# Splitting the second product of the first two down-projection units, and the last product of all by columns

## The chip, the cores and the metric

The kernel runs on one core of a Trainium2 chip. The time is device time in microseconds (us) of one execution, from three runs: median 447.69 us, 447.19 to 448.56. All matrix products are in float32.

## The reference, cut to what matters

```python
xn = layernorm(x)                       # x: (2, 1024, 512) float32
s  = s4_convolution(xn)                 # a causal convolution along the 512 features
h1 = xn @ w1.T + 2 * (xn @ A1.T) @ B1.T # 512 -> 1376, with a rank-16 addition
h3 = xn @ w3.T + 2 * (xn @ A3.T) @ B3.T
g  = silu(h1) * h3
d  = g @ w2.T + 2 * (g @ A2.T) @ B2.T   # 1376 -> 512, the down projection
out = x + s * silu(d)
```

The layer norm has no weights. The filter of the convolution is itself computed from small inputs (`Lambda`, `p`, `q`, `Vc`, `Ct`, `B`, step), a long chain of small operations.

## The kernel before, in words

The rank-16 additions are merged into the weights, so that each projection is one matrix product. Each product is done by Strassen-Winograd: a 2 by 2 block product in seven block products instead of eight, with sums of blocks made on VectorE (DVE) or GpSimd (POOL) beforehand and partial results added afterwards. The first projection (lines up to L1237) does this twice over and writes `g` to DRAM in chunks of 128 hidden rows (`store_g`, L802).

The change is in the second part, the down projection. The tokens are cut into pairs of 128 (token tiles), eight `unit`s in all (L1293). The hidden dimension has eleven chunks: ten in five pairs, and a short last one of 96 rows, `gl`. A unit makes two output tiles `o0` and `o1` of 128 tokens by 512 columns, each in two halves of 256 columns (`lo`, `hi`), from seven products. In the order of the code, by their Winograd names:

- P1 = `a11`·`b11`, into the PSUM bank `xb`, copied by ScalarE (ACT) to `z1` (L1312)
- P2 = `a12`·`b21` plus `gl`·`wl0`, into `wb`; DVE adds `z1` and gets `o0[:, lo]` (L1326)
- P6 = `s2`·`t2`, accumulated into `xb`, copied to `z2`
- P7 = `s3`·`t3` plus a product with `gl`, into `yb`
- P5 = `s1`·`t1`, accumulated into `xb`, copied to `z4`; DVE adds `yb` and gets `o1[:, hi]` (L1340)
- P3 = `s4_`·`b22` plus a product with `gl`, accumulated into `xb`, which ScalarE takes through silu into `o0[:, hi]`
- P4 = `a22`·`t4` plus a product with `gl`, accumulated into `yb`; DVE adds `z2` and gets `o1[:, lo]` (L1369)

P4 writes the bank `yb` that the addition of L1340 reads. A product of five pairs of chunks is ten matmul records of 256 columns in the profile (a float32 product has two); with `gl` it is twelve.

The engines' queues are in order, and the order is the one in which the code issues. `run` (L1386) takes the units in turn: each round advances one unit to its next `yield`, then issues one item of a list of block sums (`parts`), then, from round `s4_from` on, `s4_steps` steps of the filter's computation (`s4_work`). So a sum or a filter step that DVE gets in one round stands ahead of everything that a later round gives it. The first two units run together, with sixteen parts: the sums `t1` (two pieces), `s1` (two), `s4_` (two), `t4` (two), then eight sums for the next group of tokens, group 1, made from a load `g<-g_dram` (L1147; the tile is `g2`). The filter's steps begin with round 5, four in a round. Units 2 and 3 follow in the same way with eight steps a round; from unit 4 on the convolution (L922) is done beside the projection.

With `wait=True` (the first two units alone) P1 is issued in two parts: the first four chunks of both units, and then the fifth, because chunks 8 and 9 of `g` come from DRAM last (`room<-g_dram`). So in the kernel before, the rounds are: P1's four chunks (units 0, 1), P1's fifth chunk, P2, P6, P7, P5, P3, P4.

The last unit ends with P3 alone: after the product ScalarE takes `silu`, DVE multiplies with the convolution (L1289), adds `x` (L1290), and the half tile is stored by a DMA on SP's queue (L1291). The convolution's bank needs a late addition of `m` (L1288) before its upper half is used; `result` does it when the columns asked for end at 512.

Of the kernel before, what the change touches and what calls it, by code (L numbers as in the profile page):

```python
# [17 lines left out]
P = 128  # L18
DIM = 512
# [12 lines left out]
HALF = DIM // 2  # L32
# [75 lines left out]
def s4_gated_ffn(  # L108
# [59 lines left out]
    def bank(tag, borrow=False):  # L168

        i = turn[tag]  # L170
        if not borrow:
            turn[tag] = 1 - i
        return psum.tile([P, 512], F32, tag=f"{tag}{i}", name=tag, bufs=1)
# [571 lines left out]
    def product(ps, pairs, first, parts=1):  # L745
        n = ps.shape[1] // parts
        for part in range(parts):
            cols = slice(part * n, (part + 1) * n)
            for i, (lhsT, rhs) in enumerate(pairs):
                nc.tensor.matmul(  # L750
                    ps[:, cols],
                    lhsT=lhsT,
                    rhs=rhs if parts == 1 else rhs[:, cols],
                    start=first and i == 0 and part == 0,
                    stop=i == len(pairs) - 1,
                    skip_group_check=True,
                )
# [51 lines left out]
    class Gate:  # L809
# [12 lines left out]
        def silu(self, o, c, src):  # L822
            nc.scalar.activation(c, c if src is None else src, AF.Silu)  # L823
            self.c[o] = c
            self.pair_up()
# [89 lines left out]
    def conv_product(lhs, x01, sb, tok, tag):  # L915

        y, m_ps = bank(tag), bank("w")[:, :P]
        x0, x1, x2, x3 = (lhs[i][:, sb, k, tok] for i in range(2) for k in range(2))
        k = [conv[:, n * P : (n + 1) * P] for n in range(5)]

        def mul(to, x_, by, start=False):
            nc.tensor.matmul(  # L922
                to, lhsT=x_, rhs=by, start=start, stop=True, skip_group_check=True
            )

        mul(m_ps, x01[:, sb, tok], k[2], True)
        m = work.tile([P, P], F32, tag="m", name="m", bufs=3)
        nc.scalar.copy(m, m_ps)
        mul(y[:, : 2 * P], x0, conv[:, : 2 * P], True)
        mul(y[:, 2 * P :], x2, conv[:, : 2 * P])  # L930
        mul(y[:, 3 * P :], x0, k[3])
        mul(y[:, P : 2 * P], x1, k[0])
        mul(y[:, 2 * P : 3 * P], x1, k[4])
        mul(y[:, 3 * P :], x3, k[0])
        return y, m


    def add_chain(n, ch, places=PLACES):
# [124 lines left out]
    for n, place in enumerate((12.1, 12.8, 13.7, 14.4)):  # L1063
        b, i = divmod(n, 2)
# [84 lines left out]
    def group_piece(grp, i, sums):  # L1149


        p, n = g_in[grp][i], (3, 2)[i]
        a11, a12, a21, a22 = (
            p[:, k : k + 2 * n - 1 : 2, m] for m in range(2) for k in range(2)
        )
        s2, s3, s4_ = (sums[:, j] for j in range(3))
        parts = [
            lambda t=t, op=op: nc.vector.tensor_tensor(*t, op)
            for t, op in (
                ((s3, a11, a21), sub),  # L1160
                ((s2, a22, s3), sub),
                ((a21, a21, a22), add),
                ((s4_, a12, s2), sub),
            )
        ]
        return (a11, a12, a22, a21, s2, s3, s4_), parts

    def operands(grp, pieces):

        return [*zip(*pieces), g_in[grp][1][:LASTR, LAST - 6]]  # L1170
# [71 lines left out]
    b11, b21, _, b22 = room["b"]  # L1242
# [8 lines left out]
    class Place:  # L1251
# [30 lines left out]
                nc.sync.dma_start(out=self.o[h], in_=o_dram[self.u, h])  # L1282

        def result(self, h, y, cols=slice(0, DIM), last=False):
            o, (y, m) = self.o[h][:, cols], y
            if cols.stop == DIM:
                late = y[:, HALF:].rearrange("p (n t) -> p n t", n=2)
                nc.vector.tensor_tensor(late, late, m.unsqueeze(1).broadcast_to([P, 2, P]), add)  # L1288
            nc.vector.tensor_tensor(o, o, y[:, cols], mult)  # L1289
            (nc.vector if last else nc.gpsimd).tensor_tensor(o, o, self.xin[h][:, cols], add)  # L1290
            nc.sync.dma_start(out=out[self.rows[h], cols], in_=o)  # L1291

    def unit(u, read, held=None, wait=False):  # L1293


        a11, a12, a22, s1, s2, s3, s4_, gl = read
        pl = Place(u)
        cut, last = pl.cut, u == UNITS - 1
        xb, wb, yb = (bank(tag)[:, :HALF] for tag in ("x", "w", "y"))
        pl.gates()  # L1300
        o0, o1 = pl.o
        if u >= HOLD:
            pl.load_in()
        lo, hi = slice(0, HALF), slice(HALF, DIM)

        def mul(ps, a, b, start=False, more=()):
            chunks = [t[:, c, cut] for t in a for c in range(t.shape[1])]
            product(ps, list(zip(chunks, b)) + list(more), start)

        def snapshot(name):  # L1310
            t = work.tile([P, HALF], F32, tag=name, name=name, bufs=2)
            nc.scalar.copy(t, xb)  # L1312
            return t

        if wait:
            pairs = [t[:, c, cut] for t in a11 for c in range(t.shape[1])]
            pairs = list(zip(pairs, b11))
            product(xb, pairs[:-1], True)
            yield
            product(xb, pairs[-1:], False)  # L1320
        else:
            mul(xb, a11, b11, True)
        z1 = snapshot("z1")
        yield
        mul(wb, a12, b21, True, [(gl[:, 0, cut], wl0)])
        nc.vector.tensor_tensor(o0[:, lo], z1, wb, add)  # L1326
        if held:
            held.result(0, held.conv(0, "aux"))
        yield
        mul(xb, s2, tw[1])  # L1330
        z2 = snapshot("z2")
        silu(o0[:, lo], o0[:, lo])
        if held:
            held.result(1, held.conv(1, "aux"))
        yield
        mul(yb, s3, tw[2], True, [(gl[:, 1, cut], wl1)])
        yield
        mul(xb, s1, tw[0])
        z4 = snapshot("z4")
        nc.vector.tensor_tensor(o1[:, hi], z4, yb, add)  # L1340
        p3 = xb, s4_, b22, False, [(gl[:, 0, cut], wl1)]
        p4 = yb, a22, tw[3], False, [(gl[:, 1, cut], wld)]
        if last:
            silu(o1[:, hi], o1[:, hi])
            y = [pl.conv(0, "aux"), pl.conv(1, "aux")]
            pl.result(1, y[1], hi)
            pl.result(0, y[0], lo)
            yield
            mul(*p4)
            nc.vector.tensor_tensor(o1[:, lo], z2, yb, add)  # L1350
            silu(o1[:, lo], o1[:, lo])
            yield
            mul(*p3)
            pl.result(1, y[1], lo)
            silu(o0[:, hi], xb)
            pl.result(0, y[0], hi, True)
            return
        y0 = pl.conv(0, "aux") if u >= HOLD else None
        yield
        mul(*p3)  # L1360
        silu(o0[:, hi], xb)
        if u >= HOLD:
            y1 = pl.conv(1, "aux")
            pl.result(0, y0)
        else:
            pl.set_aside(0)
        yield
        mul(*p4)
        nc.vector.tensor_tensor(o1[:, lo], z2, yb, add)  # L1369
        silu(o1, o1)  # L1370
        if u >= HOLD:
            pl.result(1, y1)
        else:
            pl.set_aside(1)

    def sums_room():
        return work.tile([P, 3, NPAIR, JW], F32, tag="s2", name="s2", bufs=2)

    def following(grp):
        sums = sums_room()  # L1380
        two = [
            group_piece(grp, i, sums[:, :, c]) for i, c in enumerate((slice(3), slice(3, NPAIR)))
        ]
        return operands(grp, [t[0] for t in two]), two[0][1] + two[1][1]

    def run(units, parts=(), s4_steps=0, s4_from=0):  # L1386

        units, parts = deque(units), deque(parts)
        for n in itertools.count():
            while units and next(units[0], units) is units:  # L1390
                units.popleft()
            if not units:
                break
            units.rotate(-1)
            if parts:
                parts.popleft()()
            for _ in range(s4_steps if n >= s4_from else 0):
                next(s4_work, None)
        for part in parts:
            part()  # L1400
# [3 lines left out]
    two = [group_piece(0, 0, room_), group_piece(0, 1, sums_room()[:, :, 3:])]  # L1404
    read = operands(0, [t[0] for t in two])
# [3 lines left out]
    s4_loads()  # L1409
    load_g(1, range(0, NHC, 2))  # L1410
    after_, more = following(1)
    run([unit(u, read, wait=True) for u in range(2)], [*t[:2], *s1, *s4_, *t[2:], *more], 4, 5)

    second_tokens()
    lhs = [[xr[:, 0], xr[:, 1]], [room["b12"], xr[:, 2]]]
# [13 lines left out]
    read = after_  # L1429
    load_g(2, range(0, NHC, 2))  # L1430
    after_, more = following(2)
# [9 lines left out]
    for u in range(HOLD, UNITS):  # L1441
# [5 lines left out]
        if j == 0:  # L1447
            read = after_
            if ahead:
                load_g(grp + 1, range(0, NHC, 2))  # L1450
        more = ()
        if ahead and j == 1:
            after_, more = following(grp + 1)
# [77 lines left out]
```

## Time and profile before

| what | us |
|---|---|
| median of three runs | 447.69 |
| the profiled execution, its own time | 447.56 |
| its span, first to last instruction | 445.8 |
| PE (TensorE) busy in the span | 438.9 |
| DVE busy | 292.0 |
| ACT busy | 137.4 |
| POOL busy | 202.2 |

The profile is of one execution. A row of a timeline has the start and length in us, the engine, the line of the code, the operation, the tile written and the tiles read, their shape, and in brackets how long the engine stood idle before it and what ended that. PE is a matmul, PEld a weight load, which overlaps it. Rows of one kind that follow each other are merged (x4). A matmul's end is modelled and reaches into the next one's, so a rate is read from starts. The two units' first matmuls of the down projection start at 269.85 us of the span, P4 of unit 0 at 300.04, and the last product at 438.99.

### The profile page before, as it was taken

Reading aid. Unit: us, or ns where it says so; the run is one execution under the profiler, and the core shown is the slowest. Engines: PE = TensorE matmul, PEld = TensorE weight load, DVE = VectorE, ACT = ScalarE, POOL = GpSimd, SP = SyncE. Lnnn points to the kernel's source line nnn. Section 1 sums busy time; section 2 is a strip of 40 time slices with the busy share of each in tenths; the row PEclk is TensorE's granted clock in tenths of the full one; section 3 lists DMA queues with packets and bytes.
Section 4 is the critical chain, followed back from the end, with each engine's and each line's share of the span. In section 5 each row is a group of like instructions: output and inputs, shape, how many; then the busy total and the mean of one; then the engine's idle time right before and its main releaser. Section 6 shows DMA issues by size and latency. Waiting matters only on the chain.

```text
span 445.8 us, 5022 instructions
## 1 busy us (share of the span) xinstructions
PE 438.9 (98%) x1678; PEld 272.2 (61%) x1678; DVE 292.0 (66%) x496; ACT 137.4 (31%) x279; POOL 202.2 (45%) x156
## 2 busy tenths in 40 slices
PE   8999999999999999999999999999999999999996
PEld 8635334344444444444443446888898999989995
DVE  5898999946874687368836887979892214541222
ACT  2776342453245334433443242111102101011110
POOL 1315169895679548944894379200000213221221
PEclk9999999999999999999999999999999999999999
DMA  8911304025002400340054536486803742323211
GB/s 263 361 53 46 118 0 147 24 73 165 25 24 97 140 24 24 112 145 24 24 184 147 165 126 199 143 308 205 330 1 114 282 136 76 120 96 94 94 49 47
DMA packets 35257, 53.52 MB, mean 120 GB/s; under 512 B 4640, under 2 KB 21344, under 8 KB 35104
## 3 DMA queue, kind: packets, MB, share of 16 engines
q1 hardware_dynamic: 35104, 53.07, 36.2%
q8 instruction: 13, 0.21, 0.2%
q10 hardware_dynamic: 128, 0.14, 0.1%
q14 instruction: 12, 0.10, 0.1%
HBM read 33.80 MB, written 19.40 MB: 119 GB/s over the span
## 4 chain that ended last, share of the span: by engine, by line
PE 93%; DMA 2%; DVE 1%; issue 1%; POOL 1%; ACT 0%; POOLq 0%; DVEq 0%; SPq 0%
PE x L750 44%; PE y L750 23%; PE w L750 12%; PE aux L922 6%; PE w L975 2%; DMA room<-g_dram 1%; PE aux L303 1%; PE aux L381 1%; PE y L381 1%; PE w L922 1%; PE y L527 1%; PE aux L709 1%; DMA g_dram<-s 0%; POOL s L831 0%; DVE t_in L1200 0%
## 5 line engine op out<-in xcount | busy, mean ns | idle before, releaser
L1290 POOL TENSOR_TENSOR o<-o,xin 128x512 f32<-128x512 f32 (+1 forms) x17 | 22.5, 1324 | 136.9 <-DVE o L1289 136.9
L831 POOL TENSOR_TENSOR s<-c,s 128x512 f32<-128x512 f32 (+1 forms) x44 | 63.6, 1451 | 16.6 <-ACT c L823 11.5
L770 ACT COPY s<-x 128x512 f32<-128x512 f32 (+1 forms) x54 | 31.6, 586 | 87.8 <-PE x L750 86.5
L750 PE MATMUL x<-t_in,s 128*128 128x512 f32 (+1 forms) x148 | 55.2, 500 | 0.0
L774 DVE TENSOR_TENSOR s<-s,y 128x512 f32<-128x512 f32 (+1 forms) x54 | 36.1, 680 | 17.1 <-PE y L750 10.9
L864 POOL TENSOR_TENSOR s<-ua_three,s 128x512 f32<-128x512 f32 x20 | 32.4, 1619 | 26.9 <-DVE s L774 26.9
L750 PEld LDWEIGHTS x<-t_in,s 128*128 128x128 f32 x148 | 26.8, 190 | 22.8 <-issue 12.5
L864 POOL TENSOR_TENSOR ua_three<-ua_three,s 128x512 f32<-128x512 f32 x20 | 33.0, 1650 | 13.6 <-DVE s L774 13.6
L750 PE MATMUL y<-t_in,s 128*128 128x256 f32 (+1 forms) x108 | 35.9, 459 | 0.0
L1312 ACT COPY z<-x 128x256 f32<-128x256 f32 x24 | 8.8, 372 | 79.9 <-PE x L750 79.9
L864 POOL TENSOR_TENSOR s<-u_three,s 128x512 f32<-128x512 f32 x20 | 28.5, 1425 | 1.8 <-ACT c L823 1.0
L823 ACT ACTIVATE c<-c 128x512 f32<-128x512 f32 x40 | 25.2, 632 | 8.8 <-DVE c L864 8.8
L750 PEld LDWEIGHTS y<-t_in,s 128*128 128x128 f32 x108 | 20.1, 190 | 11.5 <-issue 8.8
L788 ACT COPY w<-x 128x512 f32<-128x512 f32 (+1 forms) x37 | 21.1, 570 | 12.2 <-PE x L750 12.1
L922 PE MATMUL aux<-conv,xr 128*128 128x128 f32 (+1 forms) x128 | 23.2, 314 | 0.0
L1288 DVE TENSOR_TENSOR aux<-aux,m 128x256 f32<-128x256 f32 x16 | 6.9, 431 | 23.1 <-PE aux L922 23.1
L864 POOL TENSOR_TENSOR u_three<-ua_three,u_three 128x512 f32<-128x512 f32 x10 | 12.7, 1272 | 18.3 <-DVE u_three L774 18.3
L750 PE MATMUL x<-t_in,w 128*128 128x512 f32 x40 | 20.8, 603 | 0.0
L750 PE MATMUL x<-xr,w 128*128 128x512 f32 x40 | 20.6, 614 | 0.0
L750 PE MATMUL x<-xt,w 128*128 128x512 f32 x40 | 20.6, 597 | 0.0
L750 PE MATMUL x<-xr,s 128*128 128x512 f32 x40 | 20.5, 613 | 0.0
L750 PE MATMUL x<-xt,s 128*128 128x512 f32 x40 | 20.4, 592 | 0.0
(282 smaller groups left out, 877.2 us busy)
## 6 DMA issues: line engine op xcount, KB each, us to landing
g_dram<-s SPq DMA_DIRECT2D x40, 256.0 KB, 2.1
g<-g_dram SPq DMA_DIRECT2D x10, 512.0 KB, 5.8
xin<-in_x_dram SPq DMA_DIRECT2D x16, 256.0 KB, 2.7
out_dram<-o SPq DMA_DIRECT2D x14, 256.0 KB, 2.0
t_in<-g_dram SPq DMA_DIRECT2D x6, 512.0 KB, 4.2
w<-in_w1T_dram SPq DMA_DIRECT2D x10, 256.0 KB, 4.4
w<-in_w3T_dram SPq DMA_DIRECT2D x10, 256.0 KB, 3.9
s<-in_x_dram SPq DMA_DIRECT2D x8, 256.0 KB, 4.3
```

What stands on the lines that cost most here:

```text
L381: nc.tensor.matmul(ps, lhsT=d[:, dc * P : (dc + 1) * P], rhs=h, start=start, stop=True, skip_group_check=True,)
L750: nc.tensor.matmul(ps[:, cols], lhsT=lhsT, rhs=rhs if parts == 1 else rhs[:, cols], start=first and i == 0 and part == 0, stop=i == len(pa ...
L770: nc.scalar.copy(t, self.x)
L774: nc.vector.tensor_tensor(t, t, self.y, add)
L788: nc.scalar.copy(self.w, self.x)
L823: nc.scalar.activation(c, c if src is None else src, AF.Silu)
L831: nc.gpsimd.tensor_tensor(g, act, g, mult)
L864: (nc.vector if o < 20 else nc.gpsimd).tensor_tensor(to, a, b, add)
L922: nc.tensor.matmul(to, lhsT=x_, rhs=by, start=start, stop=True, skip_group_check=True)
L975: nc.tensor.matmul(ps[:, i % 4 * P : (i % 4 + 1) * P], lhsT=ident, rhs=ident, start=first and i == 0, stop=True, skip_group_check=True,)
L1290: (nc.vector if last else nc.gpsimd).tensor_tensor(o, o, self.xin[h][:, cols], add)
L1312: nc.scalar.copy(t, xb)
```

## The change

For the first two units, P2 is cut as P1 is. The rounds become: P1's four chunks, P2's four chunks with `gl`, P1's fifth chunk, P2's fifth chunk, P6 and so on: two rounds more in all. `s4_from` goes from 5 to 6. The `parts` list is as it was.

For the last unit, P3 is done in two parts of 128 columns, each followed by its own silu, multiplication, addition and store; the store of the other tile's half stands between the products. The late addition of `m` is done at the first use of a convolution, whatever the columns.

```diff
@@ conv_product
-        return y, m
+        return [y, m, True]
@@ result
-            o, (y, m) = self.o[h][:, cols], y
-            if cols.stop == DIM:
+            o, made = self.o[h][:, cols], y
+            y, m, parts = made
+            if parts:
+                made[2] = False
                 late = y[:, HALF:].rearrange("p (n t) -> p n t", n=2)
@@ unit
         if wait:
-            pairs = [t[:, c, cut] for t in a11 for c in range(t.shape[1])]
-            pairs = list(zip(pairs, b11))
-            product(xb, pairs[:-1], True)
+            one, two = (
+                list(zip([t[:, c, cut] for t in a for c in range(t.shape[1])], b))
+                for a, b in ((a11, b11), (a12, b21))
+            )
+            product(xb, one[:-1], True)
             yield
-            product(xb, pairs[-1:], False)
+            product(wb, two[:-1] + [(gl[:, 0, cut], wl0)], True)
+            yield
+            product(xb, one[-1:], False)
         else:
             mul(xb, a11, b11, True)
         z1 = snapshot("z1")
         yield
-        mul(wb, a12, b21, True, [(gl[:, 0, cut], wl0)])
+        if wait:
+            product(wb, two[-1:], False)
+        else:
+            mul(wb, a12, b21, True, [(gl[:, 0, cut], wl0)])
         nc.vector.tensor_tensor(o0[:, lo], z1, wb, add)
@@ unit, the last one
-            mul(*p3)
-            pl.result(1, y[1], lo)
-            silu(o0[:, hi], xb)
-            pl.result(0, y[0], hi, True)
+            for n in range(2):
+                part = slice(n * P, (n + 1) * P)
+                cols = slice(HALF + n * P, HALF + (n + 1) * P)
+                chunks = [t[:, c, cut] for t in s4_ for c in range(t.shape[1])]
+                pairs = [(a, b[:, part]) for a, b in (*zip(chunks, b22), (gl[:, 0, cut], wl1))]
+                product(xb[:, part], pairs, False)
+                if n == 0:
+                    pl.result(1, y[1], lo)
+                silu(o0[:, cols], xb[:, part])
+                pl.result(0, y[0], cols, True)
             return
@@ the first two units
-    run([unit(u, read, wait=True) for u in range(2)], [*t[:2], *s1, *s4_, *t[2:], *more], 4, 5)
+    run([unit(u, read, wait=True) for u in range(2)], [*t[:2], *s1, *s4_, *t[2:], *more], 4, 6)
```

In the changed kernel the lines from L1315 on have other numbers: the additions of L1326, L1340 and L1369 are L1335, L1349 and L1384, and the multiplication and addition of `result` (L1289, L1290) are L1291 and L1292.

## The prediction

> **What bounds the kernel now.** I read the page's busy row first, then PE's waits, the chain that ended last, and then the timelines of PE and DVE around the two places that the change touches.
>
> ```profile
> PE 438.9 (98%) x1678; PEld 272.2 (61%) x1678; DVE 292.0 (66%) x496; ACT 137.4 (31%) x279; POOL 202.2 (45%) x156
> ```
>
> PE is the bound from end to end. PE's waits, in us:
>
> ```profile
> PE w L975 <- POOL ident masks.py:199: 1.4, 1, 1.4
> PE x L750 <- DMA room<-g_dram: 0.7, 1, 0.7
> ```
>
> The second row is the wait that the change aims at. On PE's timeline:
>
> ```profile
> 272.87 0.59 PE L750 MATMUL x<-w_a,room 128*128 128x256 f32 x2
> 274.15 1.13 PE L750 MATMUL x<-w_b,room 128*128 128x256 f32 x4 [0.69 <-DMA room<-g_dram]
> 275.12 1.46 PE L750 MATMUL w<-w_a,t_in 128*128 128x256 f32 x6
> ...
> 300.04 1.46 PE L750 MATMUL y<-t_in,t_in 128*128 128x256 f32 x6
> ...
> 302.64 1.46 PE L750 MATMUL y<-t_in,t_in 128*128 128x256 f32 x6
> ```
>
> Records of 256 columns start 0.216 apart (ten in 2.16 in the chain). Six records after 272.87 put P2 at 274.16; it starts at 275.12, so the wait really costs 0.96. The rows at 300.04 and 302.64 are P4 of units 0 and 1.
>
> DVE has no room to spare here. Its timeline:
>
> ```profile
> 288.54 0.95 DVE L95 TENSOR_SCALAR ex_p<-ex_p,ex_r 128x1 f32<-128x1 f32 x4
> 292.35 0.96 DVE L1158 TENSOR_TENSOR s<-g 128x768 f32<-128x768 f32 x1 [2.86 <-DMA g<-g_dram]
> 293.23 0.46 DVE L95 TENSOR_SCALAR ex_p<-ex_p,ex_r 128x1 f32<-128x1 f32 x2
> ...
> 293.93 0.95 DVE L1158 TENSOR_TENSOR s<-g,s 128x768 f32<-128x768 f32 x1
> 294.80 0.48 DVE L571 TENSOR_SCALAR room<-room,ex_out 128x512 f32<-128x512 f32 x1
> ...
> 297.23 0.41 DVE L1340 TENSOR_TENSOR o<-z,y 128x256 f32<-128x256 f32 x1
> 297.56 0.95 DVE L1158 TENSOR_TENSOR g<-g 128x768 f32<-128x768 f32 x1
> 298.43 0.68 DVE L579 TENSOR_TENSOR room<-room 128x512 f32<-128x512 f32 x1
> ...
> 301.55 0.36 DVE L1340 TENSOR_TENSOR o<-z,y 128x256 f32<-128x256 f32 x1
> 301.83 0.94 DVE L1158 TENSOR_TENSOR s<-g,s 128x768 f32<-128x768 f32 x1
> 302.69 1.76 DVE L584 RECIPROCAL den<-den 128x128 f32<-128x128 f32 x2
> 304.49 0.68 DVE L587 TENSOR_TENSOR den<-room,den 64x512 f32<-64x512 f32 x1
> ```
>
> From 292.35, when group 1's load lands, DVE works without a gap. The addition L1340 of unit 1 ends at 301.91 and P4 of unit 1, which overwrites the bank it reads, starts at 302.64: 0.73 of slack, although what it adds was there at 294.7 (the copy of `z4`). The addition of unit 0 ends at 297.64, P4 at 300.04: 2.4 of slack. These waits are not in PE's list only because they are just met. Then the end of the chain:
>
> ```profile
> 434.80 1.76 PE aux L922 x12
> ...
> 439.15 2.61 PE x L750 x12
> ...
> 441.78 0.39 ACT o L1249
> ...
> 442.19 0.43 DVE o L1289
> ...
> 442.65 0.42 DVE o L1290
> ```
>
> **P2 ahead of the late chunk.** P1's four chunks end at 273.30 (next start). Then follow P2's four chunks and `gl` for both units: 2 x 5 products x 0.431 = 4.31, to 277.61. They need chunks 1, 3, 5, 7 and the last, all loaded before chunk 8, which lands at 274.15. So that wait goes: -0.96, with 3.4 to spare. P1's fifth chunks run to 278.47, P2's to 279.34, and P6 starts at 279.35 instead of 280.31. It accumulates onto the bank that `z1` copies: unit 0's fifth chunk is through at about 278.2, the copy takes 0.4, done by 278.6; covered. The sums that P6 needs end at 276.94 and 278.61, the second of them wanted by P6's fourth pair at 280.6; covered. The PE work is the same, only ordered otherwise.
>
> **What the two rounds more do to DVE.** The parts list did not move, the units did, by two rounds; the filter by one. Counting rounds: L1340 of unit 0 was issued in round 10, after eight sums of the first set and two of group 1, and five rounds of filter steps (rounds 5 to 9). In the changed kernel it (now L1349) is in round 12, after four sums of group 1 and six rounds of filter steps (6 to 11). The built program's order says the same: ahead of it now stand `s<-g`, `s<-g,s`, `g<-g`, `s<-g,s` and the filter down to the second reciprocal of L584. All of group 1's sums wait for its load, whose place on SP's queue is as before (the order of SP's issues up to there is untouched), so 292.35 stands, and what DVE could have done before it is now less: the four L95 steps of 288.54 fall behind it. Durations from start to start, from the rows above:
>
> - 292.35: `s<-g` 0.88; four L95 0.90; `s<-g,s` 0.87; two L95, L97 and L100 0.70 (293.23 to 293.93); `g<-g` 0.87; L571 to L577 2.43 (294.80 to 297.23); `s<-g,s` 0.86 (301.83 to 302.69); L579, L581, two L584 3.12 (298.43 to 301.55). Sum 10.63: the addition of unit 0 starts at 302.98 and ends at 303.39.
> - Unit 1: 0.28 for that addition, 0.61 for the half-sized `s<-g` (the row at 305.90), two L584 1.80 (302.69 to 304.49), L587 and L589 1.41 (304.49 to 305.90): its addition starts at 307.08 and ends at 307.44.
>
> P4 in the built program waits for exactly these additions. From an engine's end to PE's next matmul the trace shows 0.1 to 0.17, say 0.12. P4 of unit 0: 303.5, where PE is ready at 299.08: a stall of 4.4. P4 of unit 1: ready at 303.5 + 2.6 = 306.1, allowed at 307.56: 1.46 more. Against 302.64 that is **+4.92**, the 0.96 won included: both starts are set by DVE, so what PE wins earlier is lost whole. Bounds: 3.9 if DVE's rows shrink by a tenth, 5.9 if they grow so or the load lands 1 later.
>
> Here a rule stands against the change. The trace's first 48 matmuls of 128x128 take 7.35 from 1.37 on, where twelve conv records later run at 0.112 for such columns: 48 x 0.112 = 5.4, so a cold start costs about 2.0. The Trainium skill ("TensorE: Matmul & The Clock Gate", section "What's actually happening") says that the array falls to half rate after an idle window of about 3.4 us, which runs freely. A gap of about 4.25 holds a whole window in one case in four. No gap of that kind is in this trace. By the rule's bad case P4 of unit 0 takes up to 2.6 more, of which unit 1's wait swallows 1.46; 0.5 on top with the 2.0 of the trace, up to 2.0 if half rate lasts into unit 1's P4. I take 0 for the likeliest and keep 2.0 for the range.
>
> **After P4.** DVE then does the rest of group 1's sums (already mostly done) and ends `wv` (L627) at about 312.7, before PE, at 314.5, asks for it (L639, one product earlier than before). The filter's last products (L690) are done near 333.4, PE's L709 wants them near 335: no new wait. Units 2 and 3 shift with PE. On SP a load of group 2 changes places with a set-aside store; DVE wants that load some 10 after its issue, the trace lands it in about 5: nothing. POOL has no instruction here.
>
> **The last product by columns.** What seems overlapped isn't: in the built program the first matmul of part 1 waits for the silu of part 0, which reads the same bank. Costs: 4 of the 12 conv records have 256 columns, so the 8 of 128 take (1.76 - 0.86) / 8 = 0.112. Part 0 ends 11 x 0.112 + 0.275 (one record's length) = 1.51 after its start; silu starts 0.03 later and takes 0.26 (as the copies of 128x128, L928); PE starts again 0.17 later, at 1.97 instead of 1.34. Part 1 needs 1.54 to its silu: 3.51, where before it was 441.78 - 438.99 = 2.79: +0.72. Behind it silu, multiplication and addition of half width save 0.12 + 0.17 + 0.13 (DVE rows of 128x128 take 0.28) = -0.42. The last store is 64 KB instead of 128 KB (1.7 to land): 0 to 0.1 less. The extra store's issue (0.33 on SP) and the early L1288 (0.43, in a DVE pause) lie under the product. Sum **+0.25**, bounds -0.1 to +0.6. The same page (section "Back-to-back issue gap") says that a stream with weight loads runs at 81 ns for 128 columns where the matmul alone takes 56, so narrow products would pay for the doubled weight loads: by that factor 24 records take 3.9 instead of 2.7, +1.2. The conv rows, same shape with one load each, show 0.112, so I leave it out.
>
> **Sum.** 447.56 (own time of the profiled execution) + 4.92 + 0.25 = 452.7; that execution is 0.13 below the median of the runs, so 452.8.
>
> **Rivals.**
> - The stall with a cold array: 453.3 to 454.8. For: the gap is longer than a window. Against: only one alignment in four, and unit 1's wait absorbs half. 0.15.
> - Not slower: the load `g<-g_dram` of group 1 decides. If it landed 4.4 earlier (by 288), DVE would start the chain before, L1349 would be met as L1340 was, and what stays is -0.96 + 0.25: 446.9. For: DVE stands idle 2.86 for it in the trace. Against: nothing moves its issue (285.51 on SP) or the traffic ahead of it. 0.05, and little of it below 446.3.
> - The change doesn't do what it says at its own place, the late chunk still stopping PE: it would land 3.4 later than shown. It would matter little, as DVE sets P4 anyway: 452.8 again. It goes with the main case.
>
> **Numbers.** Main case 0.78 (its own range 451.4 to 453.6), cold array 0.15, not slower 0.05, else 0.02. Range 451.4 to 454.8. 0.3% is 1.3 us, about what a measurement of this kernel can tell from no change (three runs spread over 1.4). Faster by over that 0.03, within 0.03, slower 0.94.
>
> **What would show it.** Right: PE's waits list `y` at L750 on DVE L1349, about 4.4 and 1.5; `room<-g_dram` is gone from it; the first L1349 near 303; silu of part 0 before PE's last twelve records, with some 0.6 idle on PE. Wrong: P4 of unit 1 starting near 302 (no DVE wait), or group 1's first `s<-g` clearly off 292.35; then the sum of the chain is what failed. Rows of P4 at twice their spacing after the gap would be the cold array.

## The result, and the profile after

| | before | after |
|---|---|---|
| median of five runs each, measured side by side | 447.96 (447.19 to 448.60) | 453.56 (453.37 to 454.53) |
| ratio of after to before, 95% interval | | 1.0131 (1.0119 to 1.0144) |
| the profiled execution: own time / span | 447.56 / 445.8 | 453.37 / 451.6 |

The changed kernel is slower by 5.6 us. The busy row of the page, after:

```profile
PE 441.6 (98%) x1690; PEld 275.0 (61%) x1690; DVE 293.0 (65%) x498; ACT 137.6 (30%) x280; POOL 201.7 (45%) x156
```

and the shares of the chain that ended last, by engine:

```profile
PE 87%; DVE 6%; DMA 3%; issue 2%; POOL 1%; ACT 0%; SPq 0%; DVEq 0%; POOLq 0%
```

PE still looks 98% busy, and as an average over the span that row hides the change. The chain does not; in the kernel before it was

```profile
PE 93%; DMA 2%; DVE 1%; issue 1%; POOL 1%; ACT 0%; POOLq 0%; DVEq 0%; SPq 0%
```

so DVE's share went from 1% to 6%. PE's longest waits say where (time in all, times, longest; counted from the modelled end of the matmul ahead):

```profile
PE y L750 <- DVE o L1349: 4.0, 1, 4.0
PE w L975 <- POOL ident masks.py:199: 1.4, 1, 1.4
PE x L750 <- ACT o L1249: 0.4, 1, 0.4
```

The wait for `room<-g_dram` is gone; in its place stands one of 4.0 for the addition L1349, and one of 0.4 for the silu between the halves of the last product. On PE's timeline of after:

```profile
278.31 1.03 PE L750 MATMUL x<-w_b,room 128*128 128x256 f32 x4
279.17 1.03 PE L750 MATMUL w<-w_b,room 128*128 128x256 f32 x4
280.03 1.46 PE L750 MATMUL x<-t_in,t_in 128*128 128x256 f32 x6
...
299.34 0.60 PE L750 MATMUL x<-w_b,room 96*128 96x256 f32 x2
303.95 2.88 PE L750 MATMUL y<-t_in,t_in 128*128 128x256 f32 x6 [4.01 <-DVE o L1349]
306.63 1.87 PE L750 MATMUL y<-t_in,room 128*128 128x256 f32 x6
308.33 1.46 PE L750 MATMUL y<-t_in,t_in 128*128 128x256 f32 x6
```

The late chunks (278.31) follow with no idle bracket. PE is ready for P4 at 299.77 (two records after 299.34) and starts at 303.95: 4.18 lost. Then something new: the first six records of P4 take 2.68 to the next row instead of 1.30, so they run at half rate, and the whole product of unit 0 takes 4.38 (303.95 to 308.33) instead of 2.60. Unit 1's P4 follows with no wait shown. DVE's timeline of after says why PE waited:

```profile
292.89 0.96 DVE L1158 TENSOR_TENSOR s<-g 128x768 f32<-128x768 f32 x1 [3.54 <-DMA g<-g_dram]
...
294.64 0.95 DVE L1158 TENSOR_TENSOR s<-g,s 128x768 f32<-128x768 f32 x1
...
296.23 0.96 DVE L1158 TENSOR_TENSOR g<-g 128x768 f32<-128x768 f32 x1
...
299.54 0.95 DVE L1158 TENSOR_TENSOR s<-g,s 128x768 f32<-128x768 f32 x1
...
303.53 0.36 DVE L1349 TENSOR_TENSOR o<-z,y 128x256 f32<-128x256 f32 x1
...
307.61 0.42 DVE L1349 TENSOR_TENSOR o<-z,y 128x256 f32<-128x256 f32 x1
```

Four sums of group 1 and the filter's steps (left out between the rows) stand between the load's landing and the first L1349: 10.64 of unbroken work, where before it was 297.23 - 292.35 = 4.88. Unit 1's addition ends at 308.03, so its P4 could not have started before about 308.15 in any case (the prediction's 0.12 from DVE's end to PE's start): the half rate lay under that second wait, and cost 0.2 in this execution.

The end of after, all engines:

```profile
444.68 1.05 PE L750 MATMUL x<-w_a,s 128*128 128x128 f32 x8
...
446.22 0.28 ACT L1249 ACTIVATE o<-x 128x128 f32<-128x128 f32 x1 [0.47 <-PE x L750]
...
446.55 1.16 PE L750 MATMUL x<-w_a,s 128*128 128x128 f32 x8 [0.37 <-ACT o L1249]
...
448.19 0.28 ACT L1249 ACTIVATE o<-x 128x128 f32<-128x128 f32 x1 [1.70 <-PE x L750]
448.50 0.29 DVE L1291 TENSOR_TENSOR o<-o,aux 128x128 f32<-128x128 f32 x1 [1.34 <-ACT o L1249]
448.82 0.29 DVE L1292 TENSOR_TENSOR o<-o,xin 128x128 f32<-128x128 f32 x1
```

The second half's matmuls wait for the first half's silu. DVE is done at 449.11, 4.43 after the product's start; before it was 443.07 - 438.99 = 4.08. So the end is 0.35 longer, of which the smaller store gives back 0.2 (1.5 to land instead of 1.7).

**The balance of the two spans** (451.6 - 445.8 = 5.8). PE's first matmul of the down projection is at 270.53 instead of 269.85: 0.68, all of it there before anything that was changed. P4 of unit 1 starts at 308.33 instead of 302.64, 5.69 later, so the change's first part costs 5.01. The last product starts at 444.68 instead of 438.99, again 5.69 later: nothing is won or lost in between. The end adds 0.35 - 0.2. Sum 5.8.

### The profile page after: what moved, and what is told of

The parts are those of the page before. It is cut to its first block, busy times and chain, and to the rows that moved or that the text cites. A ratio compares the mean times of both kernels' runs of the same rounds, so it can differ in the third digit from the quotient of the medians.

```text
span 451.6 us, 5051 instructions
## 1 busy us (share of the span) xinstructions
PE 441.6 (98%) x1690; PEld 275.0 (61%) x1690; DVE 293.0 (65%) x498; ACT 137.6 (30%) x280; POOL 201.7 (45%) x156
## 4 chain that ended last, share of the span: by engine, by line
PE 87%; DVE 6%; DMA 3%; issue 2%; POOL 1%; ACT 0%; SPq 0%; DVEq 0%; POOLq 0%
PE x L750 41%; PE y L750 22%; PE w L750 10%; PE aux L922 6%; PE w L975 2%; DMA room<-g_dram 1%; DVE s L1158 1%; DMA g<-g_dram 1%; PE aux L303 1%; PE aux L381 1%; PE y L381 1%; DVE t_in L1158 1%; PE w L922 1%; PE y L527 1%; PE aux L709 1%
## 5 line engine op out<-in xcount | busy, mean ns | idle before, releaser
L1292 POOL TENSOR_TENSOR o<-o,xin 128x512 f32<-128x512 f32 (+1 forms) x17 | 22.5, 1324 | 141.9 <-DVE o L1291 141.9
L1290 DVE TENSOR_TENSOR aux<-aux,m 128x256 f32<-128x256 f32 x16 | 6.9, 430 | 23.1 <-PE aux L922 23.1
L1249 ACT ACTIVATE o<-o 128x256 f32<-128x256 f32 (+1 forms) x17 | 8.5, 505 | 39.9 <-DVE o L1384 23.5
```

## The experiments

All are compared with the kernel before, measured beside them on the same chip; times are medians, and each trace is of one execution. **Theory**: what costs the time is the order on DVE alone. The units moved by two rounds, the list of sums not at all and the filter by one, so L1349 stands behind more work that waits for group 1's load. **Rivals**: the cut of P2 itself; half rate after the gap; the load's landing; the columns at the end.

### split_only: the cut of P2 without the columns

From after, with the last product whole again:

```diff
-            for n in range(2):
-                part = slice(n * P, (n + 1) * P)
-                ...
+            mul(*p3)
+            pl.result(1, y[1], lo)
+            silu(o0[:, hi], xb)
+            pl.result(0, y[0], hi, True)
```

> P2 is cut for the first two units as in the changed kernel, the last product stays whole. Theory (the queue order on DVE makes the loss): nearly all of the loss is here, +5.0 us on before's median of 447.96, so 452.9 to 453.3; the addition L1349 of units 0 and 1 still near 303.5 and 307.6, PE's wait for it 4 us. Rival (the column split of the last product makes a good part of the loss): 1 us or more less than the changed kernel's 453.56.

Measured: 453.15, ratio 1.0120 (1.0105 to 1.0136). The first part of the change carries the loss. PE's timeline of split_only:

```profile
303.51 2.93 PE L750 MATMUL y<-t_in,t_in 128*128 128x256 f32 x6 [3.98 <-DVE o L1349]
306.24 1.63 PE L750 MATMUL y<-t_in,room 128*128 128x256 f32 x6
307.71 1.51 PE L750 MATMUL y<-t_in,t_in 128*128 128x256 f32 x6
```

The same gap and the same half rate (2.73 for six records). This kernel, without the second part, is the base of most of what follows.

### tail_only: the columns without the cut

The kernel before, with the last product and `result` as in the changed kernel:

```diff
-            mul(*p3)
-            pl.result(1, y[1], lo)
-            silu(o0[:, hi], xb)
-            pl.result(0, y[0], hi, True)
+            for n in range(2):
+                ...
+                product(xb[:, part], pairs, False)
+                if n == 0:
+                    pl.result(1, y[1], lo)
+                silu(o0[:, cols], xb[:, part])
+                pl.result(0, y[0], cols, True)
```

> Only the last product is cut in two parts of 128 columns, P2 and the order as before. Theory: +0.2 to +0.4 us on before's median (448.2 to 448.4), with the silu of part 0 standing between the two parts (PE idle 0.4 to 0.6) and the end of the work after the last matmul about 0.4 shorter. Rival (the parts overlap and the shorter end is kept): -0.3.

Measured: 447.88 against 447.83, ratio 1.0005 (0.9995 to 1.0015). The interval holds no change and +0.25 alike, and leaves out a gain of 0.3. The trace shows the same wait of PE for ACT as after did, and 4.44 from the product's start to DVE's end. The second part of the change is worth a few tenths at most.

### order_alone: DVE's order of after, with P2 whole

The kernel before, with the first two sums issued ahead of the units and the rest of the list and the filter moved up, so that what stands ahead of the additions is as in the changed kernel:

```diff
-    run([unit(u, read, wait=True) for u in range(2)], [*t[:2], *s1, *s4_, *t[2:], *more], 4, 5)
+    for part in t[:2]:
+        part()
+    run([unit(u, read, wait=True) for u in range(2)], [*s1, *s4_, *t[2:], *more], 4, 4)
```

> The kernel before with P2 whole; DVE alone gets the order of the changed kernel: the first two sums are issued ahead of the rounds, so that every sum stands two rounds earlier against the units, and the filter starts with round 4 instead of 5, one round earlier against the units (as in the changed kernel). Theory (the order, not the split products, makes the stall, and DVE sets the start of P4 whatever PE has won): P4 of unit 1 near 307.6 to 308.3, time within 0.3 us of split_only, 452.7 to 453.3, though the wait for the late chunk is back. Rival (it is the split of P2 that costs, by its own waits on PE): 448.0, as before.

Measured: 452.73, ratio 1.0109 (1.0092 to 1.0126). PE's waits in order_alone:

```profile
PE y L750 <- DVE o L1340: 3.0, 2, 1.7
PE w L975 <- POOL ident masks.py:199: 1.4, 1, 1.4
PE x L750 <- DMA room<-g_dram: 1.1, 1, 1.1
```

P2 is not cut, the late chunk still stops PE, and the loss is there all the same: the order on DVE is enough. The profiled execution was the shortest of its six runs (451.44). In it group 1's load landed early, at 291.21, and P4 of unit 1 started at 306.41 instead of the expected 307.6 to 308.3; the first addition stands 10.65 behind the landing, at 301.86, as in after. Whether the other five were longer because their load landed later is not known; they have no trace.

### order_kept: P2 cut, DVE's order as before

From split_only, with the sums and the filter moved down with the units:

```diff
-    run([unit(u, read, wait=True) for u in range(2)], [*t[:2], *s1, *s4_, *t[2:], *more], 4, 6)
+    run([unit(u, read, wait=True) for u in range(2)], [*[lambda: None] * 2, *t[:2], *s1, *s4_, *t[2:], *more], 4, 7)
```

> P2 cut as in the changed kernel, last product whole, and the order on DVE kept as in before: two empty items ahead of the sums and the filter from round 7. Theory: no wait of 4 us at P4; the late chunk's wait of 0.96 gone; the additions end at 297.6 and 301.9 as in before and PE reaches P4 of unit 1 at 301.7, so 0.35 of it is lost again: 447.96 - 0.6 = 447.3 to 447.5. Rival (the order isn't it): 452 and more.

Measured: 447.16, ratio 0.9984 (0.9975 to 0.9993). Neither `room<-g_dram` nor L1349 is in PE's list of waits. DVE's timeline of order_kept:

```profile
292.36 0.96 DVE L1158 TENSOR_TENSOR s<-g 128x768 f32<-128x768 f32 x1 [2.67 <-DMA g<-g_dram]
...
297.23 0.41 DVE L1349 TENSOR_TENSOR o<-z,y 128x256 f32<-128x256 f32 x1
...
301.56 0.36 DVE L1349 TENSOR_TENSOR o<-z,y 128x256 f32<-128x256 f32 x1
```

The additions stand 4.87 and 9.20 behind the landing, as before. P4 of unit 1 starts at 301.97, with PE ready at 301.89, against 302.64 in the kernel before: 0.67 earlier, or 0.88 counted from the first matmul of the down projection (270.06 here, 269.85 before). The times say 0.67 (447.83 - 447.16). So the cut of P2 is worth about 0.7 once the order is kept. Keeping the order takes 5.99 us off split_only (453.15 - 447.16), with the same PE work.

### filter_late and parts_late: which of the two it is

Both from split_only. filter_late starts the filter as order_kept does and leaves the sums early; parts_late does the opposite:

```diff
 filter_late
-    run(..., [*t[:2], *s1, *s4_, *t[2:], *more], 4, 6)
+    run(..., [*t[:2], *s1, *s4_, *t[2:], *more], 4, 7)
 parts_late
-    run(..., [*t[:2], *s1, *s4_, *t[2:], *more], 4, 6)
+    run(..., [*[lambda: None] * 2, *t[:2], *s1, *s4_, *t[2:], *more], 4, 6)
```

> As split_only (P2 cut, last product whole), but the filter starts with round 7, so that it stands against the units as in before; the sums stay two rounds earlier. Theory (what stands in DVE's queue behind the load of group 1 and ahead of the additions sets P4, to be counted row by row): behind the load at 292.4 then stand four sums, 3.48, and the filter from L86 to L577, 4.73, so the addition of unit 0 starts 8.2 after the load instead of 10.6, that of unit 1 at about 304.6, P4 of unit 1 at 305.1: +2.4 on before, 450.3. Rival (it is the sums alone, or the filter alone): 453.1 or 447.2.

> As split_only, but the sums are moved back by two rounds, so that they stand against the units as in before; the filter stays one round earlier (round 6). Theory, by the same count: behind the load then stand two sums, 1.75, and the filter's two rounds L571 to L584, 5.55, so the addition of unit 0 starts 7.3 after the load, that of unit 1 ends near 304.4, P4 of unit 1 at 304.5: +1.9, 449.7. Rival as before: 453.1 or 447.2.

Measured: filter_late 449.70, ratio 1.0040 (1.0025 to 1.0055); parts_late 449.79, ratio 1.0046 (1.0031 to 1.0062). The rows of both that count, on DVE; first filter_late:

```profile
291.62 0.96 DVE L1158 TENSOR_TENSOR s<-g 128x768 f32<-128x768 f32 x1 [3.96 <-DMA g<-g_dram]
...
299.80 0.41 DVE L1349 TENSOR_TENSOR o<-z,y 128x256 f32<-128x256 f32 x1
```

and parts_late:

```profile
292.34 0.96 DVE L1158 TENSOR_TENSOR s<-g 128x768 f32<-128x768 f32 x1 [1.85 <-DMA g<-g_dram]
...
299.65 0.36 DVE L1349 TENSOR_TENSOR o<-z,y 128x256 f32<-128x256 f32 x1
```

From landing to first addition: 4.87 with both in the old order, 8.18 with the sums early (3.31 more), 7.31 with the filter early (2.44 more), and 10.63 with both in split_only (5.76 more, against 3.31 + 2.44 = 5.75). On DVE the two add up within 0.01. filter_late's time is 0.6 under the expected 450.3; its load landed at 291.62 where 292.4 was expected. In time, each kernel against the kernel before that was measured beside it: order_kept -0.67, filter_late +1.72, parts_late +1.81, split_only +5.32, so that each alone costs 2.4 to 2.5 and both together 6.0. Both are to blame, in about equal shares. That the pair costs 1.1 more than the sum is not explained by the chain. The load's landing, where it begins, lies between 291.21 and 293.13 over the traces with its issue in the old place, and no run separates that. Half rate may have a part in it: of these four kernels only split_only has it, and kept_warm, the next run, takes it away and is 5.00 instead of 5.32 above the kernel before, a difference within the intervals.

### kept_warm: the half rate taken away

From split_only, with 17 products of the identity ahead of unit 0's P4:

```diff
+            if u == 0:
+                keep_warm(bank("aux", True), 17, True)
             mul(*p4)
```

> As split_only, with 17 idle products of 128x128 (34 records, about 3.8 us) on PE ahead of P4 of unit 0, into a free bank, while it waits; nothing reads them. In split_only P4 of unit 0 ran at half rate after the gap (4.2 instead of 2.6 us). Theory (DVE's second addition sets P4 of unit 1 near 307.7 either way, and the half rate lies under that wait): P4 of unit 0 takes 2.6, P4 of unit 1 waits about 1.5 for DVE, time within 0.4 of split_only's 453.15. Rival (the cold array costs by itself): about 1.6 less, 451.5.

Measured: 452.98, ratio 1.0110 (1.0096 to 1.0124), which overlaps split_only's interval; the 451.5 that the rival expected (ratio 1.008) is outside. PE's timeline of kept_warm:

```profile
300.07 3.96 PE L975 MATMUL aux<-ident 128*128 128x128 f32 x34
304.19 1.56 PE L750 MATMUL y<-t_in,t_in 128*128 128x256 f32 x6 [0.16 <-DVE o L1349]
305.59 1.46 PE L750 MATMUL y<-t_in,room 128*128 128x256 f32 x6
308.35 1.56 PE L750 MATMUL y<-t_in,t_in 128*128 128x256 f32 x6 [1.30 <-DVE o L1349]
```

Now P4 of unit 0 runs at full rate (1.40 to the next row), and what it saves comes back as a wait of 1.30 for unit 1's addition. The granted clock of each kernel by stretches (stretch; its length; PE's busy time and records; granted clock; DMA share; GB/s), in split_only:

```profile
300.00:312.00 12.00, 8.48 (x32) 0.86 0.48 160
```

and in kept_warm:

```profile
300.00:312.00 12.00, 10.54 (x65) 1.00 0.61 198
```

The slowdown of P4 was the clock, granted at 0.86 over these 12 us (in after too), and giving it back in full buys nothing that the times show: DVE sets both starts. In split_only's trace P4 of unit 1 starts 0.11 behind the end of its addition (307.18 + 0.42), so there the half rate cost nothing at all.

### load_first: the load two microseconds earlier

From split_only, with the load of group 1 issued by SP behind the first of the filter's small loads instead of behind all of them (its line numbers are one higher):

```diff
         nc.sync.dma_start(out=par, in_=s4_par)
+        load_g(1, range(0, NHC, 2))
         ...
     s4_loads()
-    load_g(1, range(0, NHC, 2))
```

> As split_only, but on SP's queue the load g<-g_dram of group 1 is issued right after par, ahead of the small loads vc, bp and hcol, which took 2.6 us of issue before it. DVE's order is that of split_only. Theory (the landing of that load starts a chain of fixed length on DVE: 10.63 us to the addition of unit 0, 15.2 to P4 of unit 1 in the four traces so far): the load lands about 2.6 earlier, near 289.8, where DVE is ready at about 289.4, P4 of unit 1 at 305.0, 2.6 less than split_only: 450.4 to 450.8. Rival (DVE's work itself, not the load, is the limit, or the later small loads stop L595 on PE and what hangs on it): 452.5 and more.

Measured: 450.67, ratio 1.0066 (1.0054 to 1.0078). DVE's timeline of load_first:

```profile
290.85 0.96 DVE L1159 TENSOR_TENSOR s<-g 128x768 f32<-128x768 f32 x1 [1.63 <-DMA g<-g_dram]
...
301.58 0.36 DVE L1350 TENSOR_TENSOR o<-z,y 128x256 f32<-128x256 f32 x1
```

SP issues it 2.28 earlier (283.57 instead of 285.85), and it lands 1.62 earlier than in split_only. The first addition is 10.73 behind it, as before within 0.1, so the two P4 start 1.51 and 1.57 earlier (302.00 and 306.14). Counted from the first matmul of the down projection (270.41 here, 270.13 in split_only) the landing is 1.90 earlier and P4 of unit 1 1.85. Each against the kernel before that was measured beside it, the loss is 3.22 (450.67 - 447.45) instead of 5.32 (453.15 - 447.83), 2.1 less. So the landing is the start of the chain, as the theory has it, and an earlier load wins back four tenths of the loss. That the time fell into the expected 450.4 to 450.8 is partly luck: the landing was expected 2.6 earlier and P4 of unit 1 at 305.0. The half rate went too (mean clock 0.998 to 1.000 in all six runs), and no run here tells what of the 2.1 is due to that. It isn't free: PE has a new wait of 1.5 (`aux` at L596 for `bp_sb<-in_bp_dram`, one of the loads pushed back), which here lies under DVE's.

### two_banks: both parts of the change, with the two waits mended

From order_kept, with the last product by columns, but its first half in the other `x` bank, which DVE adds to `z4`, so that nothing in the second half's bank is read while it is written:

```diff
+            late = bank("x")[:, :P]
+            for n, ps in enumerate((late, xb[:, P:])):
+                ...
+                product(ps, pairs, n == 0)
+                if n == 0:
+                    pl.result(1, y[1], lo)
+                    nc.vector.tensor_tensor(o0[:, cols], z4[:, part], ps, add)
+                    silu(o0[:, cols], o0[:, cols])
+                else:
+                    silu(o0[:, cols], ps)
+                pl.result(0, y[0], cols, True)
```

> As order_kept (P2 cut, DVE's order kept), and the last product in two parts of 128 columns, of which the first goes into another PSUM bank: DVE adds it to the copy z4, so that the second part, in the old bank, has no silu to wait for. Theory: PE runs through (24 records at 0.112, 2.7 us), half-width silu, multiplication and addition behind the last matmul save 0.4, the smaller store 0.2: about 0.5 below order_kept's 447.16, 446.6 to 446.8. Rival (a narrow product costs more on PE than the shorter end saves): 447.2 or more.

Measured: 446.98, ratio 0.9977 (0.9969 to 0.9985). The end of two_banks, all engines:

```profile
438.74 1.05 PE L750 MATMUL x<-w_a,s 128*128 128x128 f32 x8
...
440.08 1.06 PE L750 MATMUL x<-w_a,s 128*128 128x128 f32 x8
...
441.62 0.28 ACT L1249 ACTIVATE o<-x 128x128 f32<-128x128 f32 x1 [0.71 <-PE x L750]
```

PE goes through without a wait, and DVE is done at 442.54, 3.80 after the product's start, where the whole product takes 4.08 and the columns in one bank 4.43. This is the fastest version run, 1 us under the kernel before. The time lies between the 446.6 to 446.8 of its theory and the 447.2 of the rival, so the times don't decide; the lead over order_kept, 0.2 to 0.3, shows in the trace but lies within the intervals of the times.

## Why the prediction was right

Predicted was 452.8 (451.4 to 454.8) and slower with a chance of 0.94; measured 453.56. The mechanism, DVE's order setting P4, was right. The number alone could not show that: 453.56 is at the top of the main case's own range (451.4 to 453.6) and inside that of the rival with the cold array (453.3 to 454.8), whose sign, rows of P4 at twice their spacing, did appear. What separates the two is order_kept and kept_warm.

- **P2 ahead of the late chunk, -0.96.** Right: P6 starts at 280.03, and without the 0.68 by which this execution was late already, at 279.35. That it is lost whole as long as DVE sets P4 is right too; order_kept keeps about 0.7 of it.
- **The chain from the load to the additions.** Predicted 10.63, measured 10.64; in split_only, order_alone, kept_warm and load_first 10.63, 10.65, 10.64 and 10.73. That it can be added up from rows of the trace before is shown by its parts: taking out the sums or the filter steps shortens it by what their rows say. order_alone and order_kept show that this order is cause enough without the cut, and that the cut without the order costs nothing. The bounds of 3.9 and 5.9 were too narrow for what they name: P4 of unit 1 hangs on both stretches of the chain, 10.63 and 4.10, so rows longer or shorter by a tenth move it by 1.5 and not by 1.
- **The two waits, 4.4 and 1.46, less the 0.96 won: 4.92.** The sum was right (5.01 in the trace), the list of waits not: it shows 4.0 once. The second wait was filled by P4 of unit 0 running at half rate. Landing to P4 of unit 1 was predicted as 307.56 - 292.35 = 15.21 and is 15.24 in split_only and 15.22 in kept_warm; after's 15.44 contains the 0.2 that the half rate costs beyond that wait.
- **The cold array.** Here the weighing was wrong. The prediction's one case in four for a gap of 4.25 was an estimate from the freely running idle window of about 3.4 us in the Trainium skill ("TensorE: Matmul & The Clock Gate", section "What's actually happening"). The profiled gaps of 4.18 in after and 4.14 in split_only both ended in half rate, and the mean granted clock was 0.992 to 0.995 in all five runs of after and all four of split_only, but 0.999 or 1.000 in kept_warm's four. So, as far as the mean clock tells, it comes every time here. In the two traces most of it goes under unit 1's wait, and the price was 0.2 and 0 where that rival had 0.5 to 2.0. It can be higher: two runs of after and two of split_only had 0.992 instead of 0.995, which over 452 us is some 2.7 us more at half rate (an estimate, from rounded means), and took on average 0.4 and 0.7 longer than the others. None of those four has a trace.
- **The last product by columns, +0.25.** In the trace right: silu of the second half 3.51 after the start (predicted 3.51), the end +0.35 instead of +0.30, the store -0.2 where 0 to 0.1 was allowed. The first eight narrow records took 0.89 (444.68 to 445.57), 0.111 each, so the 1.2 that was weighed for the doubled weight loads did not come. The times alone can't tell the whole from nothing (tail_only).
- **The rest.** Nothing happens between P4 and the last product, as predicted. The rival "the load decides" was not what took place, but load_first shows its mechanism: a landing 1.62 earlier gives P4 1.5 earlier.
- **The 0.8 above the point.** The kernel before itself was 0.27 higher beside the changed one than in the three runs behind the prediction (447.96 and 447.69), and the half rate is another 0.2 in the trace. The remaining 0.3 is less than a kernel's own runs spread (about 1 between lowest and highest) and stays unexplained.

## What to carry to other kernels

When work is split into more steps of a round-robin schedule, everything else that the rounds hand out moves relative to it: count, for each in-order queue, what now stands ahead of the instruction whose result the engine that sets the time needs. A wait of one engine for another that is just met is in no list of waits; its slack (here 0.73) has to be read from two rows of the timelines, before a queue is reordered. Splitting a product so that its first part could be used early helped here only where the second part wrote a bank that the reader of the first didn't hold, and then by 0.3 in the trace.

## What the runs showed of the hardware

- **Half rate after a gap.** Matmul records of 256 columns ran 0.447 apart (after) and 0.455 (split_only) instead of 0.216, after PE had stood for 4.18 and 4.14 us. The clock granted over 12 us was 0.86 in both, which is half of full speed for about 3.4 us (12 x 0.14 / 0.5). After gaps of 0.7 to 1.9 us (filter_late, parts_late, load_first, order_alone's profiled execution) no row ran so (the first six records took 1.40 to the next row, against 1.30 without a gap). order_alone's other five runs have a mean clock of 0.995 or 0.996 and its profiled one 0.999; what gap they had is not known. Where between 1.9 and 4.1 the limit lies was not tried.
- **The start varies by more than the differences sought.** The first 48 matmuls, the same in every kernel, took 7.35 in the trace before; PE's timeline of after has

```profile
1.37 8.32 PE L975 MATMUL w<-ident 128*128 128x128 f32 x48 [1.37 <-POOL ident masks.py:199]
```

  and over the traces it lies between 7.05 (tail_only) and 8.50 (kept_warm). So after lost 0.97 there against before, of which 0.68 was left at the first matmul of the down projection; why the stretch varies was not tried. So two single profiles must be compared from a common later event, not from the span's start.
- **A load issued 2.28 earlier landed 1.62 earlier**, and PE then had a new wait of 1.5 for one of the loads pushed back behind it. Why the landing doesn't follow the issue in full was not tried.
